# Weight rows in front of the merges, row blocks by turns and in-place combinations in a one-core adaLN kernel

## The chip, the cores and the metric

The kernel runs on one core of one Trainium2 chip. The metric is the device time of one execution in microseconds (us), given as a median of several executions. Lower is better.

## The reference

One adaLN layer over x of 4 batches x 1024 rows x 2048 columns, in float32. A modulation of six parts is made from a small vector, each part a 2048 x 2048 block of `wmod` ("a section"). A long convolution over the columns (a state-space kernel K with a skip term D), and then a linear layer whose weight is W plus sixteen LoRA updates, each stand between a layer norm with scale and shift and a gated residual.

```
mod = (silu(c) @ wmod).reshape(4, 6, 1, 2048)
sa, ca, ga, sb, cb, gb = six parts of mod            # sections 0 to 5
ga, gb = sign(g) * max(|g|, 0.25)
h = layernorm(x) * (1 + ca) + sa
x = x + ga * (causal_conv(h, K) + D * h)             # K from the state-space parameters
h = layernorm(x) * (1 + cb) + sb
x = x + gb * (h @ W.T + bias + sum_e coeffs_e * scales_e * (h @ A_e.T) @ B_e.T)
```

The inputs are random; some are scaled up by fixed factors.

## The kernel before

The work has three stretches. **Set-up**: K is computed and written as Toeplitz blocks, and sections 1, 0 and 2 of the modulation are made. **Convolution**: 16 groups of 256 rows (two row blocks of 128). **Linear layer**: two halves q of output columns by 16 units of 256 rows, with a seven-product scheme (Strassen-Winograd form), whose seven weight combinations were merged with the LoRA product and stored to a scratch tensor `wcd` during the convolution. Every matmul operand is split into a high and a low float16 part, and three of the four products are taken.

The program is written in order, and a framework then fixes at build time which instruction stands where in each engine's queue. It may move a ready instruction ahead of an earlier one that it expects to wait, and program order is the priority. On the chip each queue runs in its order. All large loads and stores are issued by SyncE's queue (SP).

**Modulation rows.** A section is 16 rows (L816 to L835): `mod_load` (L314) loads a [128, 2048] float32 tile of 1 MiB, tag `wm`, in a pool of three buffers (`WM, WMS = 3, 3`, L781), and `mod_mm` (L320) does four matmuls with it into one PSUM tile. A seventeenth step turns the sum into a column or gate. Each of these matmuls shows as two records in the trace, so a row is 8.

**LoRA preparation.** `prep_lora` (L385) loads A (`la`, 2 MiB) and then B (`lb`, 2 MiB) into the one buffer `we`, takes norms with ScalarE squares whose element output is junk (`lsq`, L412, tag `wct`), and writes the float16 factors `lbh` and `lbl` (L421 to L424).

**Merges.** `merge` (L429) does one of eight column chunks in 15 steps. Eight steps each make a PSUM tile `lps` of six matmuls (L448) and add it to the loaded weight on VectorE (L450). Squares (L458, junk `wsq` in `wct`), a power-of-two scale and two scaling steps follow. Then seven combinations of the quarters b11, b12, b21, b22 are written by `put` (L472): a ScalarE cast, a VectorE subtraction for the low part (L476), and a store from `wch`, of two buffers. One combination goes through an own tile `wct` (L483).

**Convolution of a group.** `conv_mm` (L552) goes over the output halves q = 0, 1 and in each over the row blocks r = 0, 1. For each it runs three `family` calls (L560): family 0 into `ya`, which ScalarE copies to `qs` (L585, one buffer); family 2 into `yb`, which VectorE adds to `qs` (L589) and gates (L591); and family 1 on top of `ya`, which VectorE gates (L597) and adds to the residual (L604). A family has 12 matmuls for q = 0 (512, 384, 256 and 128 columns, three each: "short") and 24 for q = 1 ("long"). `ya`, `yb` and `lps` share five PSUM tiles (`ACC = 5`, L772).

**Fill order.** Between families `tick()` is called, 18 times a group; `PLAN` (L775) says what comes at each. "S" takes one step of the generator `rest` (L884), from group 1 on. "P" and "Q" are the store and statistics of a finished row block (`conv_post`, L616), "T" and "N"/"O" prepare the next group (`stats`, `conv_prep` L521). The order inside `rest` is:

```
mods = (x for sec in (4, 3, 5) for x in section(sec, (wmp,)))
n = 0
for _ in mer:          # prep_lora, then eight merges
    yield
    n += 1
    if n % MR == 0:    # MR = 2
        next(mods, None)
        yield
for _ in mods:
    yield
```

So step 0 of group 1 is the LoRA preparation, step 1 the first merge matmuls, step 2 the first row of section 4. When `rest` is used up, its pools are closed (L916). Group 0 has no gate while it is convolved; the gate tile is made after it (L979) and `conv_late` (L608) applies it on VectorE, followed by the two stores `x1d` of `conv_post`.

Of the kernel before, what the change touches and what calls it, by code (L numbers as in the profile page):

```python
# [12 lines left out]
F32 = mybir.dt.float32  # L13
F16 = mybir.dt.float16
BF16 = mybir.dt.bfloat16
# [4 lines left out]
MUL, ADD, SUB = ALU.mult, ALU.add, ALU.subtract  # L20
# [4 lines left out]
P = 128  # L25
# [9 lines left out]
class Net:  # L35
# [349 lines left out]
    def prep_lora(self, pool, tmp):  # L385
        nc, v, io = self.nc, self.nc.vector, self.io
        ws = pool.tile([P, 2, 2], F32, tag="lws", name="lws")
        for i, n in enumerate(("coeffs", "scales")):
            x = io[n]
            for k in range(2):  # L390
                src = bass.AP(tensor=x.tensor, offset=x.offset + 8 * k, ap=[[1, 8], [0, 16], [1, 1]])
                nc.sync.dma_start(out=ws[:, i, k : k + 1], in_=src)
        a = tmp.tile([P, 2, D], F32, tag="we", name="la")
        nc.sync.dma_start(out=a, in_=io["A"].rearrange("c p k h d -> p c k (h d)"))

        am = pool.tile([P, 2], F32, tag="lam", name="lam")
        av = a.rearrange("p k d -> p (k d)").rearrange("p (c k d) -> p k c d", c=HC, k=2)
        for k in range(2):
            nc.scalar.activation(av[:, k], av[:, k], AF.Square, accum_out=am[:, k : k + 1])
        nc.scalar.activation(am, am, AF.Sqrt)  # L400
        sa, ia = self.pow2(pool, am, 2, "lsa")
        wt = pool.tile([P, 2], F32, tag="lwt", name="lwt")
        v.tensor_tensor(wt, ws[:, 0, :], ws[:, 1, :], MUL)
        v.tensor_tensor(wt, wt, ia, MUL)
        self.lsa = sa
        b = tmp.tile([P, 2, D], F32, tag="we", name="lb")
        nc.sync.dma_start(out=b, in_=io["BfT"].rearrange("(k p) o -> p k o", p=P))
        b4 = pool.tile([P, 4], F32, tag="lb4", name="lb4")
        for k in range(2):
            nc.scalar.activation(b[:, k], b[:, k], AF.Copy, scale=wt[:, k : k + 1])  # L410
            for h in range(2):
                j = tmp.tile([P, 1024], F32, tag="wct", name="lsq")  # L412
                i = 2 * k + h
                nc.scalar.activation(j, b[:, k, ds(1024 * h, 1024)], AF.Square, accum_out=b4[:, i : i + 1])
        bm = pool.tile([P, 1], F32, tag="lbm", name="lbm")
        v.tensor_reduce(bm, b4, AX.X, ADD)
        nc.scalar.activation(bm, bm, AF.Sqrt)
        sb, self.linv = self.pow2(self.cst, self.allmax(pool, bm, 1, "lbm"), 1, "lsb")
        self.bh = pool.tile([P, 2, D], F16, tag="lbh", name="lbh")
        self.bl = pool.tile([P, 2, D], F16, tag="lbl", name="lbl")  # L420
        for k in range(2):  # L421
            nc.scalar.activation(b[:, k], b[:, k], AF.Copy, scale=sb)
            nc.scalar.copy(self.bh[:, k], b[:, k])  # L423
            v.tensor_tensor(self.bl[:, k], b[:, k], self.bh[:, k], SUB)  # L424
        self.winv = self.const("winv", [P, NC])
        self.wcd = self.dram.tile([2, 7, P, HC, 2, 512], F16, tag="wcd", name="wcd")


    def merge(self, pool, tmp, c):  # L429
        nc, v = self.nc, self.nc.vector  # L430
        lf = tmp.tile([P, 2, 2, P], F32, tag="laf", name="laf")
        nc.sync.dma_start(out=lf, in_=self.io["A"][c])
        la = tmp.tile([P, 2, 2, 2, P], F16, tag="lac", name="lac")
        for k in range(2):
            v.tensor_scalar(lf[:, k], lf[:, k], self.lsa[:, k : k + 1], None, MUL)
        nc.scalar.copy(la[:, 0], lf)
        v.tensor_tensor(la[:, 1], lf, la[:, 0], SUB)
        we = tmp.tile([P, 2, D], F32, tag="we", name="we")
        for h in range(2):
            nc.sync.dma_start(out=we[:, h], in_=self.io["WT"][ds(P * (c + HC * h), P), :])  # L440
        for h in range(2):
            for q in range(4):
                ps = self.acc.tile([P, 512], F32, tag="a", name="lps")
                osl = ds(512 * q, 512)
                n = 0
                for k in range(2):
                    for x, y in ((0, self.bh), (0, self.bl), (1, self.bh)):
                        nc.tensor.matmul(ps, la[:, x, k, h], y[:, k, osl], start=(n == 0), stop=(n == 5))  # L448
                        n += 1
                v.scalar_tensor_tensor(we[:, h, osl], ps, self.linv, we[:, h, osl], MUL, ADD)  # L450
                yield

        m = pool.tile([P, 4], F32, tag="wem", name="wem")
        for h in range(2):
            for q in range(2):
                j = tmp.tile([P, 1024], F32, tag="wct", name="wsq")
                i = 2 * h + q
                nc.scalar.activation(j, we[:, h, ds(1024 * q, 1024)], AF.Square, accum_out=m[:, i : i + 1])  # L458
        mm = pool.tile([P, 1], F32, tag="wmm", name="wmm")
        v.tensor_reduce(mm, m, AX.X, ADD)  # L460
        nc.scalar.activation(mm, mm, AF.Sqrt)
        s, inv = self.pow2(pool, mm, 1, "wes")
        for h in range(2):
            v.tensor_copy(self.winv[:, c + HC * h : c + HC * h + 1], inv)
            for q in range(2):
                sl = ds(1024 * q, 1024)
                nc.scalar.activation(we[:, h, sl], we[:, h, sl], AF.Copy, scale=s)
            yield
        b11, b12 = we[:, 0, 0:1024], we[:, 0, 1024:2048]
        b21, b22 = we[:, 1, 0:1024], we[:, 1, 1024:2048]  # L470

        def put(i, t):  # L472
            hl = tmp.tile([P, 2, 2, 512], F16, tag="wch", name="wch", bufs=2)
            tv = t.rearrange("p (q n) -> p q n", n=512)
            nc.scalar.copy(hl[:, :, 0, :], tv)
            v.tensor_tensor(hl[:, :, 1, :], tv, hl[:, :, 0, :], SUB)  # L476
            STQ(nc).dma_start(out=self.wcd[:, i, :, c].rearrange("q p h n -> p q h n"), in_=hl)

        put(0, b11)
        put(1, b21)  # L480
        yield
        put(2, b22)
        t1 = tmp.tile([P, 1024], F32, tag="wct", name="wct")  # L483
        v.tensor_tensor(t1, b12, b11, SUB)
        put(4, t1)
        yield
        v.tensor_tensor(b12, b22, b12, SUB)
        put(6, b12)
        yield
        v.tensor_tensor(b11, b12, b11, ADD)  # L490
        put(5, b11)
        yield
        v.tensor_tensor(b21, b21, b11, SUB)
        put(3, b21)
        yield

# [55 lines left out]
    def conv_mm(self, pl, hs, xs, std, tick, early, out):  # L552

        nc, v = self.nc, self.nc.vector
# [19 lines left out]
                if i == 3 and q == 1:  # L574
                    tick()

        for q in range(2):
            for r in range(2):
                y = ys[r]
                yv = y.rearrange("p (j e t) -> p j e t", e=2, t=P)  # L580
                jj = slice(4 * q, 4 * q + 4)
                pa = self.acc.tile([P, 4, P], F32, tag="a", name="ya")
                family(pa, 0, q, r, True)
                qs = pl["q"].tile([P, 4, P], F32, tag="qs", name="qs")
                nc.scalar.copy(qs, pa)  # L585
                tick()
                pb = self.acc.tile([P, 4, P], F32, tag="a", name="yb")
                family(pb, 2, q, r, True)
                v.tensor_tensor(yv[:, jj, 1, :], pb, qs, ADD)  # L589
                if not early:  # L590
                    v.tensor_tensor(yv[:, jj, 1, :], yv[:, jj, 1, :], gv[:, jj, 1, :], MUL)  # L591
                tick()
                family(pa, 1, q, r, False)
                if early:
                    nc.scalar.copy(yv[:, jj, 0, :], pa)
                else:
                    v.tensor_tensor(yv[:, jj, 0, :], pa, gv[:, jj, 0, :], MUL)  # L597
                    self.residual(xs[r], ys[r], std[:, r : r + 1], sums[r], q)
                tick()

    def residual(self, x, y, std, sums, q):

# [165 lines left out]


ORDER = (0, 4, 5, 1, 6, 2, 3)  # L770
MR = 2
ACC, TPS = 5, 2  # L772


# [20 lines left out]
def net(ctx: ExitStack, tc: tile.TileContext, io):  # L795
    nc = tc.nc
# [12 lines left out]
    pl = {}  # L809
# [73 lines left out]
        pl[name] = pool(left, "p1" + name, bufs)  # L883
    def rest():  # L884
        mods = (x for sec in (4, 3, 5) for x in section(sec, (wmp,)))
        n = 0
        for _ in mer:
            yield
            n += 1
            if n % MR == 0:  # L890
# [4 lines that stand above are left out]
        k.ginv = k.fold_scale(msm, k.cb, k.sb, "fs2", k.winv)  # L895
        yield
# [179 lines left out]
```

## Time and profile before

| | us |
|---|---|
| Median of 3 executions | 2163.01 |
| Lowest, highest | 2156.66, 2166.04 |
| The profiled execution | 2160.88 |
| Its span, first to last instruction | 2159.1 |
| TensorE (PE) busy | 2070.2 |
| VectorE (DVE) busy | 1273.2 |
| ScalarE (ACT) busy | 912.2 |

The profile is of one execution. Its times count from the start of the span. PE is TensorE's matmuls and PEld its weight loads; SPq is SP's queue, whose lines are DMA issues and not the movement itself. Its part 2 cuts the span in 40 slices of 54 us with a digit for the busy tenths, and PEclk is the granted TensorE clock in tenths. A line of the order of time has start, duration, engine, source line, operation, output and inputs, count, and in brackets the idle time before it and what ended that.

Groups 1 to 15 of the convolution run from about 167 to 945 us, the linear layer from there to the end.

### The profile page before, as it was taken

How to read it: one execution, taken by the hardware profiler on the slowest of the kernel's cores; microseconds unless marked ns; L12 is line 12 of the kernel's file. 1: busy time of each engine (PE TensorE's matmuls, PEld its weight loads, DVE VectorE, ACT ScalarE, POOL GpSimd, SP SyncE). 2: the span in 40 equal slices, each digit the busy share in tenths (PEclk: the TensorE clock that was granted, in tenths of full speed). 3: DMA queues.
4: the chain of work that ended last, by engine and by line, in shares of the span. 5: the costliest groups of instructions: out<-in, count | busy, mean ns of one | idle time of the engine just before them, and what ended most of it. 6: DMA issues, size and time to landing. Idle time of an engine off the chain costs nothing.

```text
span 2159.1 us, 27722 instructions
## 1 busy us (share of the span) xinstructions
PE 2070.2 (96%) x11084; PEld 1020.6 (47%) x11084; DVE 1273.2 (59%) x2037; ACT 912.2 (42%) x1267; POOL 2.7 (0%) x12
## 2 busy tenths in 40 slices
PE   5696999999999999999999999999999999999999
PEld 1143554545445555654555555545444444444444
DVE  6537778887788877765666566565533323232323
ACT  1246666666667666654555454554200000000000
POOL 0000000000000000000000000000000000000000
PEclk8797999999999999999999999999999999999999
DMA  9987577876775442397556465465695545555542
GB/s 399 379 294 292 209 284 277 306 260 246 280 293 183 173 158 98 127 360 275 218 214 217 173 225 214 169 244 192 248 345 183 185 156 171 169 165 167 175 153 72
DMA packets 127130, 483.00 MB, mean 224 GB/s; under 512 B 13670, under 2 KB 13799, under 8 KB 96023
## 3 DMA queue, kind: packets, MB, share of 16 engines
q1 hardware_dynamic: 126464, 479.65, 61.7%
q8 instruction: 87, 1.43, 0.3%
q10 hardware_dynamic: 538, 1.59, 0.2%
q14 instruction: 41, 0.34, 0.0%
HBM read 325.89 MB, written 155.30 MB: 223 GB/s over the span
## 4 chain that ended last, share of the span: by engine, by line
PE 62%; issue 25%; DVE 7%; DMA 3%; ACT 3%; SPq 0%; POOL 0%; POOLq 0%; DVEq 0%; ACTq 0%
PE fZ L712 23%; PE fX L712 15%; PE fY L712 15%; PE ya L569 3%; PE tp L662 3%; PE yb L569 2%; PE modps L322 1%; DVE h L549 1%; ACT x L622 1%; DVE y L604 1%; ACT h L548 1%; DMA xo<-x1d 1%; DVE s4wr L177 1%; DMA w<-wcd 1%; DVE st L513 1%
## 5 line engine op out<-in xcount | busy, mean ns | idle before, releaser
L712 PEld LDWEIGHTS <-lf 128*128 128x128 f16 x5376 | 525.8, 98 | 620.2 <-issue 0.5
L712 PE MATMUL fZ<-w,lf 128*128 128x512 f16 x2304 | 514.0, 379 | 0.2 <-ACT p L720 0.2
L569 PEld LDWEIGHTS <-h 128*128 128x128 f16 x3456 | 319.7, 98 | 317.1 <-issue 69.1
L569 PE MATMUL ya<-kh,h 128*128 128x512 f16 (+3 forms) x1536 | 380.5, 328 | 8.2 <-ACT qs L585 5.1
L712 PE MATMUL fY<-w,lf 128*128 128x512 f16 x1536 | 343.1, 379 | 0.0
L712 PE MATMUL fX<-w,lf 128*128 128x512 f16 x1536 | 342.5, 379 | 0.0
L569 PE MATMUL ya<-kl,h 128*128 128x512 f16 (+3 forms) x768 | 251.5, 328 | 0.0
L731 DVE SCALAR_TENSOR_TENSOR xo<-xo,mv,gb 128x512 f32<-128x512 f32 x128 | 95.2, 750 | 248.7 <-DMA xo<-x1d 236.7
L569 PE MATMUL yb<-kh,h 128*128 128x512 f16 (+3 forms) x768 | 192.2, 326 | 0.0
L720 ACT COPY p<-fZ 128x512 f32<-128x512 f32 x64 | 37.3, 582 | 292.5 <-PE fZ L712 275.0
L322 PE MATMUL modps<-wm,sct 128*32 128x512 f32 x768 | 116.5, 677 | 43.1 <-DMA wm<-in_wmod 34.0
L664 ACT ACTIVATE gt<-tp,sb,cb 128x256 f32<-128x256 f32 x256 | 123.9, 570 | 63.7 <-PE tp L662 62.1
L720 ACT COPY p<-fX 128x512 f32<-128x512 f32 x32 | 18.7, 586 | 303.9 <-PE fX L712 240.2
L542 ACT ACTIVATE t<-tp,sa,ca 128x256 f32<-128x256 f32 x256 | 126.2, 565 | 32.3 <-PE tp L539 23.4
L549 DVE TENSOR_TENSOR h<-t,h 128x1536 f16<-128x1536 f32 x64 | 112.2, 1754 | 28.2 <-ACT h L548 27.7
L569 PE MATMUL yb<-kl,h 128*128 128x512 f16 (+3 forms) x384 | 125.2, 326 | 0.0
L548 ACT CAST h<-t 128x1536 f16<-128x1536 f32 x64 | 94.1, 1470 | 26.2 <-DVE t L547 26.2
L736 DVE TENSOR_TENSOR fin<-fX,gb 128x512 f32<-128x512 f32 x32 | 22.1, 692 | 125.8 <-PE fX L712 125.7
L448 PE MATMUL lps<-lbh,lac 128*128 128x512 f16 x256 | 87.2, 382 | 6.4 <-ACT lbh L423 5.1
L675 DVE TENSOR_TENSOR lf<-gt,lf 128x1024 f16<-128x1024 f32 x64 | 76.7, 1220 | 18.3 <-ACT lf L674 18.2
L513 DVE BATCH_NORM_STATS2 st<-x 128x6 f32<-128x512 f32 x128 | 83.3, 681 | 5.1 <-DMA x<-in_x 5.1
L539 PE MATMUL tp<-ident,x 128*128 128x128 f32 x512 | 73.0, 279 | 12.8 <-ACT t L542 6.9
(236 smaller groups left out, 1863.1 us busy)
## 6 DMA issues: line engine op xcount, KB each, us to landing
wm<-in_wmod SPq DMA_DIRECT2D x96, 1024.0 KB
lfd<-lf SPq DMA_DIRECT2D x112, 512.0 KB
lf<-lfd SPq DMA_DIRECT2D x112, 512.0 KB
x<-in_x SPq DMA_DIRECT2D x32, 1024.0 KB
x1d<-y SPq DMA_DIRECT2D x32, 1024.0 KB
x<-x1d SPq DMA_DIRECT2D x32, 1024.0 KB
xo<-x1d SPq DMA_DIRECT2D x128, 256.0 KB
out<-xo SPq DMA_DIRECT2D x128, 256.0 KB
```

Source lines behind the costliest of these rows:

```text
L322: self.last = self.nc.tensor.matmul(self.modps[32 * g : 32 * g + 32, :], self.sct[:, j].rearrange("p r b -> p (r b)"), w[:, ds(512 * g, 512)],
L448: nc.tensor.matmul(ps, la[:, x, k, h], y[:, k, osl], start=(n == 0), stop=(n == 5))
L513: v.bn_stats(st[:, q], xs[r][:, ds(512 * q, 512)])
L539: nc.tensor.transpose(tp[:, c, r], xs[r][:, ds(P * (4 * k + 2 * i + c), P)], self.ident)
L542: nc.scalar.activation(t[:, 2 * i + c], tp[:, c], AF.Identity, bias=self.sa[:, d, b : b + 1], scale=self.ca[:, d, b : b + 1],)
L548: nc.scalar.copy(h[:, 0], t)
L549: v.tensor_tensor(h[:, 1], t, h[:, 0], SUB)
L569: nc.tensor.matmul(pf[:, o:512], h[:, x], self.kf[f][z][:, ds(k0, 512 - o)], start=first, stop=(i == last and (x, z) == (1, 0)), skip_grou ...
L664: nc.scalar.activation(t[:, c0 + c], tp[:, c], AF.Identity, bias=self.sb[:, c0 + c, b : b + 1], scale=self.cb[:, c0 + c, b : b + 1],)
L675: v.tensor_tensor(hl[:, :, 1, :], s, hl[:, :, 0, :], SUB)
L712: nc.tensor.matmul(ps[name], lf[i][:, k, x, :], wc[i][k // 4][:, k % 4, y, :], start=(first and n == 0), stop=(n == 3 * HC - 1), skip_grou ...
L731: v.scalar_tensor_tensor(x, x, m, self.gbias[:, h], ADD, ADD)
```

## The change

Six edits, which come together:

1. `rest` takes ten rows of section 4 first. After the seventh it takes one step of the merge generator, which is the LoRA preparation.
2. After that one row follows three merge steps, not two (`MR` 3).
3. In the half q = 0, the two row blocks take turns: family 0 of both, family 2 of both, family 1 of both. Half q = 1 keeps its order. The number of ticks stays 18. `qs` has a buffer for each row block.
4. The combinations are made in place in b12 and b11, and the tile `wct` of 4 KiB a partition goes. Products 5 and 6 are stored in the other order.
5. The junk of the squares goes to bfloat16 views of `wch` tiles.
6. The pool of weight tiles has three buffers, as it had.

```diff
-                j = tmp.tile([P, 1024], F32, tag="wct", name="lsq")
+                j = tmp.tile([P, 2, 2, 512], F16, tag="wch", name="lsq", bufs=2)
+                j = j.rearrange("p q h n -> p (q h n)").bitcast(BF16)[:, 0:1024]
...
-        t1 = tmp.tile([P, 1024], F32, tag="wct", name="wct")
-        v.tensor_tensor(t1, b12, b11, SUB)
-        put(4, t1)
+        v.tensor_tensor(b12, b12, b11, SUB)
+        put(4, b12)
         yield
         v.tensor_tensor(b12, b22, b12, SUB)
-        put(6, b12)
-        yield
-        v.tensor_tensor(b11, b12, b11, ADD)
-        put(5, b11)
-        yield
-        v.tensor_tensor(b21, b21, b11, SUB)
+        put(5, b12)
+        yield
+        v.tensor_tensor(b11, b12, b11, SUB)
+        put(6, b11)
+        yield
+        v.tensor_tensor(b21, b21, b12, SUB)
         put(3, b21)
...
-        for q in range(2):
-            for r in range(2):
...
+        def begin(q, r):
+            pa = self.acc.tile([P, 4, P], F32, tag="a", name="ya")
+            family(pa, 0, q, r, True)
+            qs = pl["q"].tile([P, 4, P], F32, tag=f"qs{r}", name="qs")
+            nc.scalar.copy(qs, pa)
+            tick()
+            return pa, qs
...
+        ps = [begin(0, r) for r in range(2)]
+        for r in range(2):
+            odd(0, r, ps[r][1])
+        for r in range(2):
+            even(0, r, ps[r][0])
+        for r in range(2):
+            pa, qs = begin(1, r)
+            odd(1, r, qs)
+            even(1, r, pa)
...
-MR = 2
+MR, MOD0 = 3, 10
...
         mods = (x for sec in (4, 3, 5) for x in section(sec, (wmp,)))
+        for n in range(MOD0):
+            if n == MOD0 - 3:
+                next(mer)
+                yield
+            next(mods)
+            yield
         n = 0
```

`odd` and `even` hold the statements of families 2 and 1 as they were, and the squares of the merges (`wsq`) get the same edit as `lsq`.

More of the change, by code (lines that the diff above doesn't have):

```diff
@@ L455, in merge @@
             for q in range(2):
-                j = tmp.tile([P, 1024], F32, tag="wct", name="wsq")
+                j = tmp.tile([P, 2, 2, 512], F16, tag="wch", name="wsq", bufs=2)
+                j = j.rearrange("p q h n -> p (q h n)").bitcast(BF16)[:, 0:1024]
                 i = 2 * h + q
@@ L575, in family @@
                     tick()
-        for q in range(2):
-            for r in range(2):
[L579 to L599, printed above, removed]
+        def begin(q, r):
[5 more added lines that the diff above has]
+            return pa, qs
@@ new lines, in odd, with even @@
+        def odd(q, r, qs):
+            yv, jj = ys[r].rearrange("p (j e t) -> p j e t", e=2, t=P), slice(4 * q, 4 * q + 4)
+            pb = self.acc.tile([P, 4, P], F32, tag="a", name="yb")
+            family(pb, 2, q, r, True)
+            v.tensor_tensor(yv[:, jj, 1, :], pb, qs, ADD)
+            if not early:
+                v.tensor_tensor(yv[:, jj, 1, :], yv[:, jj, 1, :], gv[:, jj, 1, :], MUL)
+            tick()
+        def even(q, r, pa):
+            yv, jj = ys[r].rearrange("p (j e t) -> p j e t", e=2, t=P), slice(4 * q, 4 * q + 4)
+            family(pa, 1, q, r, False)
+            if early:
+                nc.scalar.copy(yv[:, jj, 0, :], pa)
+            else:
+                v.tensor_tensor(yv[:, jj, 0, :], pa, gv[:, jj, 0, :], MUL)
+                self.residual(xs[r], ys[r], std[:, r : r + 1], sums[r], q)
+            tick()
```

## The prediction

> **What bounds the kernel now.** I read the busy shares and the slices first, then a table by stretches, then PE's waits, then the order of time on PE and on SP's queue at the one hole. Page, parts 1 and 2:
>
> ```profile
> PE 2070.2 (96%) x11084; PEld 1020.6 (47%) x11084; DVE 1273.2 (59%) x2037; ACT 912.2 (42%) x1267; POOL 2.7 (0%) x12
> ...
> PE   5696999999999999999999999999999999999999
> ...
> PEclk8797999999999999999999999999999999999999
> ```
>
> TensorE is the bound: 2070 of 2159 us, and nearly all of the other 89 us lies in the first four slices (54 us each). Slices 1 to 3 are fed by the weight rows of sections 1, 0 and 2, which the change doesn't touch. The fourth (162 to 216 us) is its subject. The stretches around it, as us of busy time per engine, then granted clock and DMA share:
>
> ```profile
> 167.00:177.90 10.90, 10.86 (x74) 5.57 (x72) 10.87 (x16) 6.56 (x11) 0.00 (x0) 1.00 0.93 362
> 177.90:199.80 21.90, 1.93 (x3) 0.29 (x4) 16.03 (x46) 19.78 (x23) 0.40 (x1) 0.57 0.87 348
> 199.80:206.00 6.20, 6.20 (x22) 2.82 (x22) 5.53 (x9) 2.96 (x4) 0.00 (x0) 0.60 0.15 24
> ...
> 400.00:690.00 290.00, 282.76 (x1750) 147.20 (x1749) 240.01 (x419) 195.19 (x269) 0.00 (x0) 1.00 0.71 261
> 690.00:945.00 255.00, 246.02 (x1537) 143.34 (x1536) 199.46 (x370) 169.11 (x230) 0.38 (x1) 1.00 0.45 166
> ```
>
> One hole of 21.9 us with 1.93 us of PE work; later PE is 97% busy. Its two causes, on PE:
>
> ```profile
> 175.08 2.78 PE L322 MATMUL modps<-wm,sct 128*32 128x512 f32 x24
> 192.81 1.92 PE L322 MATMUL modps<-wm,sct 128*32 128x512 f32 x2 [14.95 <-DMA wm<-in_wmod]
> 199.79 0.58 PE L448 MATMUL lps<-lbh,lac 128*128 128x512 f16 x1 [5.06 <-ACT lbh L423]
> 200.17 0.63 PE L569 MATMUL ya<-kh,h 128*128 128x512 f16 x1
> ```
>
> Three rows of section 4 run (24 records), the fourth waits 15 us for its load, then the first merge matmul waits 5 us for the LoRA factor lbh. Behind both, in queue order, stands group 1's second row block (200.17), whose inputs had long been ready. Why the fourth row came late, on SP's queue:
>
> ```profile
> 170.50 0.38 SPq L407 DMA_DIRECT2D lb<-in_BfT  x1
> 176.07 4.59 SPq L618 DMA_DIRECT2D x1d<-y  x2
> 180.76 2.56 SPq L502 DMA_DIRECT2D x<-in_x  x2
> 183.41 0.99 SPq L317 DMA_DIRECT2D wm<-in_wmod  x2
> ```
>
> Its slot was not free before the rows of 175.08 had run, and SP then stood at group 0's stores (the second waits for DVE until 180.3) and x loads. The other PE waits, whole run:
>
> ```profile
> PE ya L569 <- ACT qs L585: 5.1, 8, 1.8
> PE lps L448 <- ACT lbh L423: 5.1, 1, 5.1
> PE ya L569 <- DVE y L589: 2.8, 1, 2.8
> ...
> PE lps L448 <- DVE y L589: 1.3, 1, 1.3
> ```
>
> The qs waits (5.1 here; the page's group of L569 has 8.2 us of idle in all) are what taking turns aims at. The two on DVE y L589 look like waits for a PSUM tile to be emptied.
>
> **What the Trainium skill says.** "PSUM — Partial Sum Buffer", section "Engine vs sequencer instructions": matmuls start and complete in program order, and the ScalarE and VectorE queues are strict FIFO. The trace agrees: ready matmuls stood 20 us behind one row. "TensorE: Matmul & The Clock Gate", section "What's actually happening": after an idle window of about 3.4 us the array runs at half clock until it has been busy about as long. The trace has 0.57 in the hole and 0.60 in the 6.2 us after it. "DMA: Bandwidth & Descriptors", section "Issuing engines are not separate DMA queues": all queues share the same 16 engines, so loads compete. Here the share is 0.93 at 362 GB/s before the hole. "Perfetto Trace Analysis", section "Identifying Performance Opportunities", takes regular gaps as a possible sign of too few PSUM buffers. Here they are few: 10 us of 442 from 248 to 690.
>
> **The change part by part.** The sum is made against the profiled execution: 2160.9 us (span 2159.1 and 1.8 around it); the median of three, 2163.0, lies 2.1 above.
>
> *Rows in front of the merges.* In front of the first merge matmul the fill order now has seven rows, the LoRA preparation, then three rows; that matmul becomes step 11 of group 1, not step 1. What the hole costs today: 20.0 us idle, plus 6.2 x 0.40 = 2.5 us at half clock after it, plus 0.9 us because the row at 192.81 took 1.9 us where one takes 1.0 at full clock: **23.4 us**.
>
> What PE can run there: a short family takes 1.73 us (173.35 to 175.08). Group 1's second block has three: 5.2 us. Its long families (24 matmuls) take 4.2 us (217.82 to 222.04) and may start when the last h piece is written, 182.8; three of them give 12.6 us. Seven rows (3 to 9) give 7 us. The sum, 24.8 us, covers 20. No work is added: the 48 rows are all loaded anyway.
>
> What stays is whether the rows arrive. With 10.9 us of work as now up to 177.9, 5.2 of short families, 3 for rows 3 to 5, two long families 8.4, rows 6 to 8, a transpose piece 0.9 and half a family 2.6, PE wants row 9 at about 201. From 157 on DMA has to move 10 rows, lb (2 MB), two x1d and two x tiles, each of 1 MiB: 16 x 1.05 = 16.8 MB, at 362 GB/s 46 us, so until 203: 2 us short. And the rows pass SP's queue behind the x1d stores and x loads (176.07 to 183.41, 7.3 us): I take half, 4 us. Row 0 now runs earlier, after the first short family, so its slot frees about 169, and some reloads get ahead of the stores. Residual wait **+6**, bounds 0 (all in time) and 13.2 (row 3 still lands at 192.8 and PE reaches it at 177.9 + 1.73 = 179.6). Half clock after shorter waits: **+1.5**, bounds 0 and 3.4, today's.
>
> The LoRA chain (la square at 166.6, lb load at 170.5, ACT at 182.87 to 199.7) keeps its instructions; its step moves from 0 to 7, so its six loads on SP, ACT's some 20 instructions and one POOL reduction rank behind more group 1 work. lbh at 200 to 205 is hidden as PE reaches the merges only past 201: 0; without that cover up to +5.
>
> *Merges by threes.* With one row after three merge steps (was two) a group's 18 steps hold 13.5 merge steps, not 12. A merge costs DVE (46.0 + 57.6 + 9.8 + 39.0 + 5.5 + 5.3)/8 = 20.4 us for its lines L450, L476, L484 to L493, L437, L435, so 1.36 per step and +2.0 us per group. A group takes about 49 us with DVE 83% busy (240 of 290): it becomes 87%. PE is the later engine, so this is hidden; it costs only where PE waits for DVE. The fill ends after 173 steps, not 182, still in front of group 15 where it is needed: 0.
>
> *Turns in the short half.* Same matmuls, same 18 ticks. Family 1 of a block now stands three short families, 5.2 us, behind its qs copy (0.58 us), not one: its wait goes. Half of the 8.2 us are from long families or other causes: **-3**, bounds 0 and -8. The price is PSUM: ya and yb of both blocks, four of five accumulators, are open at once, so merges have one or two tiles, not three. lps (1.3 us) and its DVE pass (0.74) recur every tick of about 3 us, so one tile is enough unless DVE's queue is late. With the denser merges I take **+4**, bounds 0 and +38 (two waits of 2.1 us, the mean of the two DVE y waits above, in 8.9 groups).
>
> *In place, and squares into wch.* The operation count is the same. b12 is written again only after put(4) has read it (1.04 ACT + 1.22 DVE), one step later anyway: 0; without cover 2.3 us x 8 = 18 us on DVE, not on PE. The squares write 2-byte junk: ACT's 1057 ns stay. They take slots whose last store stands on SP ahead of the next weight load (274.14 against 274.55): no new wait. The second qs tile takes no time.
>
> **Sum:** -23.4 + 6 + 1.5 - 3 + 4 = -14.9 us: 2146.0 for a profiled execution, 2148 with the 2.1.
>
> **Rivals.**
> *Rows still late.* SP keeps today's order, row 3 lands at 192.8: 13.2 us of the hole stay, with today's half-clock cost, and later rows lose 2 us as their slots free late. Gain 20.0 - 13.2 = 6.8, less 2; with the -3 and +4 that leaves 3.8: 2157.1, so **2159**. For it: DMA at 0.93 and SP standing at 176 to 183. Against: row 0's earlier turn.
> *PSUM and DVE, slower.* In the short halves PE waits for a tile twice a group, 2.1 us each, in 8.9 groups with merges: +37.4. With the other terms (-18.9): 2179.4, so **2181**. For it: four open accumulators, DVE at 87%. Against: two such waits today in all, 4.1 us. It gets slower by over 0.5% from 29.7 us, 3.3 us a group.
> *Nothing left.* The hole closes but lbh is late by 5 and PSUM waits take 12: so -23.4 + 6 + 1.5 - 3 + 5 + 12 = -1.9: **2161**.
>
> **How the numbers follow.** Forecast 0.55 with all that is faster by over 0.5%; late rows 0.18 and nothing left 0.10, both within 0.5%; slower 0.17. A measurement of this kernel tells about 0.5% (10.8 us) from no change, so faster is below 2152.2. The range: low 2134, all of 23.4 and some qs waits gained; high 2174, the edge of no change; outside stay the slower rival's 0.17 and 0.03 below.
>
> **What would show it.** Right: no PE gap over 6 us past 178; a short family of the second block straight after the first's; the first lps past 200; clock 1.0 from 200 to 206; no qs waits in short halves. Wrong: a row waiting over 10 us for wm; lps or ya waiting for DVE y more than ten times; PE under 97% from 248 to 690.

## The result and the profile after

| us | before | after |
|---|---|---|
| Median (20 executions each) | 2162.27 | 2166.34 |
| Lowest to highest | 2156.66 to 2166.04 | 2163.73 to 2170.0 |
| The profiled execution, its span | 2160.88, 2159.1 | 2163.73, 2161.9 |
| First gate matmul to first matmul of the linear layer, same profiles | 772.7 | 772.2 |

The ratio is 1.0021 with an interval of 1.0014 to 1.0029: slower by about 4 us, and within the 0.5% that the prediction called no change. It forecast 2148. The last row is the convolution (`gps`, the gate tile's first matmul, at 165.73 and 169.33; `fX` at 938.45 and 941.53). It is 0.5 us shorter. The profile's 2.8 us more lie ahead of it, where the gate came 3.6 us later. In the profiles of the kernels below the gate comes anywhere from 166.05 to 171.18, without a clear link to the edits, so I judge the change by the convolution and by the medians. The convolution is known from one profiled execution of each kernel, and that execution lies up to some 5 us from the kernel's median (2168.69 against 2173.94 in one case below); differences of a few us between convolutions alone say little.

Parts 1 and 2 of the page after:

```profile
PE 2080.0 (96%) x11084; PEld 1022.9 (47%) x11084; DVE 1271.9 (59%) x2037; ACT 912.3 (42%) x1267; POOL 4.1 (0%) x12
...
PE   5699899999999999999999999999999999999999
...
PEclk8699999999999999999999999999999999999999
```

The fourth slice has gone from 6 to 9, as forecast, and its clock from 7 to 9. The fifth (216 to 270 us) has gone from 9 to 8. The table by stretches (busy us of PE, PEld, DVE, ACT, POOL, then clock, DMA share, GB/s) shows the exchange. First the changed kernel, then two stretches of the kernel before:

```profile
177.90:199.80 21.90, 21.90 (x146) 10.71 (x144) 19.61 (x42) 10.96 (x15) 0.00 (x0) 1.00 0.97 364
199.80:206.00 6.20, 5.34 (x36) 1.97 (x35) 5.61 (x17) 2.48 (x3) 0.00 (x0) 1.00 1.01 424
206.00:216.00 10.00, 6.43 (x32) 2.89 (x36) 1.76 (x9) 10.00 (x11) 0.00 (x0) 0.66 1.03 420
216.00:248.00 32.00, 23.21 (x112) 10.48 (x105) 19.43 (x28) 22.55 (x31) 1.86 (x1) 0.84 0.64 243
...
400.00:690.00 290.00, 282.52 (x1714) 147.26 (x1713) 244.28 (x421) 198.73 (x275) 0.00 (x0) 1.00 0.71 265
690.00:945.00 255.00, 246.84 (x1554) 143.18 (x1553) 200.25 (x369) 167.12 (x225) 0.38 (x1) 1.00 0.42 153
```

```profile
206.00:216.00 10.00, 10.00 (x57) 5.21 (x56) 6.01 (x9) 4.72 (x5) 0.00 (x0) 1.00 0.47 197
216.00:248.00 32.00, 32.00 (x194) 16.85 (x195) 18.12 (x35) 20.38 (x32) 0.00 (x0) 1.00 0.40 140
```

The old hole, 178 to 200, is full. A new one stands behind it: PE is idle for 0.86 + 3.57 + 8.79 = 13.2 us from 199.8 to 248, and its clock drops to 0.66 and 0.84, which by the table's own figures costs an estimated 6.43 x 0.34 + 23.21 x 0.16 = 5.9 us. In the kernel before, the stretches 206 to 248 were busy throughout at full clock. So 23.4 us became 19.1, a gain of 4.3, of which the convolution shows 0.5.

Most of the rest went into the rows themselves. From the gate to the linear layer PE is idle for 7.0 us less than before (32.0, not 39.0), but with the same number of matmul records it is busy for 6.5 us more (740.2, not 733.7). The 48 rows take 59.0 us of this, where they took 53.7. Most of the reason shows in the first row of section 4 in the changed kernel:

```profile
174.54 1.04 PE L322 MATMUL modps<-wm,sct 128*32 128x512 f32 x2
175.52 1.09 PE L540 MATMUL tp<-ident,x 128*128 128x128 f32 x8
176.54 1.06 PE L322 MATMUL modps<-wm,sct 128*32 128x512 f32 x6
```

A row's four matmuls write four different groups of 32 partitions of one PSUM tile, and here they overlap: a whole row (8 records) takes 1.07 us, its first matmul alone (2 records) 1.04, the other three (6 records) 1.06. Where the order that was fixed at build time puts other matmuls behind the first one, the row costs a microsecond more. Two rows are split in this way in the kernel before and seven in the changed one; five more are an estimated 5 us. No run changes these splits alone.

From 400 on the shares of the stretches hardly moved. PE's order of time in the new hole:

```profile
203.95 1.07 PE L322 MATMUL modps<-wm,sct 128*32 128x512 f32 x8
205.88 0.44 PE L540 MATMUL tp<-ident,x 128*128 128x128 f32 x2 [0.86 <-ACT x L529]
207.87 0.88 PE L540 MATMUL tp<-ident,x 128*128 128x128 f32 x6 [1.55 <-ACT x L529]
210.76 2.02 PE L540 MATMUL tp<-ident,x 128*128 128x128 f32 x8 [2.02 <-ACT t L543]
212.72 4.38 PE L322 MATMUL modps<-wm,sct 128*32 128x512 f32 x24
222.09 2.02 PE L540 MATMUL tp<-ident,x 128*128 128x128 f32 x8 [4.99 <-ACT t L543]
...
230.41 0.58 PE L449 MATMUL lps<-lbh,lac 128*128 128x512 f16 x1 [3.59 <-ACT lbh L424]
```

By 205 PE has run nine of group 1's twelve families and seven of the ten rows. What comes next in its order is group 2's transposes, which need group 2's normalised x (L529) and whose PSUM tiles ScalarE empties (t, L543), with the other three rows among them (212.72), and then the first merge matmul, which wants lbh. Only behind that stand the last three long families of group 1. Before, the first such transposes ran at 228.9, behind 29 us of families and merge matmuls. The three rows at 212.72 take 4.38 us at the lower clock; 24 such records took 2.78 us at 175.08 before. What ScalarE does meanwhile:

```profile
203.73 4.08 ACT L529 ACTIVATE x<-x,nb,rs 128x2048 f32<-128x2048 f32 x2 [1.30 <-DVE nb L519]
...
211.60 3.90 ACT L410 ACTIVATE lb<-lb,lwt 128x2048 f32<-128x2048 f32 x2
...
219.55 1.47 ACT L549 CAST h<-t 128x1536 f16<-128x1536 f32 x1
...
224.67 3.90 ACT L423 ACTIVATE lb<-lb,lsb_s 128x2048 f32<-128x2048 f32 x2
228.47 3.69 ACT L424 CAST lbh<-lb 128x2048 f16<-128x2048 f32 x2
```

The 16 us block for B (two scaling passes, four squares, a cast, from 211.60) stands between the copies out of PSUM that the transposes wait for, and lbh's cast is reached at 228.47. It doesn't explain all of PE's waits: the first three, 0.86 + 1.55 + 2.02 = 4.4 us, end before the block starts, while ScalarE is normalising group 2's x and squaring a finished block (L637, 207.72). The wait of 4.99, one of 0.21 after it and the 3.59 for lbh, 8.8 us in all, stand behind it. Before, the block ran while PE stood in the old hole, and the x of group 2 came after it:

```profile
182.87 1.99 ACT L410 ACTIVATE lb<-lb,lwt 128x2048 f32<-128x2048 f32 x1
...
197.86 3.68 ACT L423 CAST lbh<-lb 128x2048 f16<-128x2048 f32 x2
...
205.44 4.08 ACT L528 ACTIVATE x<-x,nb,rs 128x2048 f32<-128x2048 f32 x2
```

Link by link the LoRA chain fell behind: A's load from 151.87 to 166.71 (+14.8), its first square from 166.57 to 179.85 (+13.3), B's load from 170.50 to 190.59 (+20.1), B's scaling from 182.87 to 211.60 (+28.7), the cast +30.6. In each of these, 3.6 us are the later gate of this profile.

### The profile page after: what moved, and what is told of

Same layout as the page of the kernel before. It is cut to its first block, busy times and chain, and to the rows that moved or that the text cites. A ratio compares the mean times of both kernels' runs of the same rounds, so it can differ in the third digit from the quotient of the medians.

```text
span 2161.9 us, 27708 instructions
## 1 busy us (share of the span) xinstructions
PE 2080.0 (96%) x11084; PEld 1022.9 (47%) x11084; DVE 1271.9 (59%) x2037; ACT 912.3 (42%) x1267; POOL 4.1 (0%) x12
## 4 chain that ended last, share of the span: by engine, by line
PE 64%; issue 23%; DVE 8%; ACT 3%; DMA 2%; ACTq 0%; POOL 0%; POOLq 0%; SPq 0%; DVEq 0%
PE fZ L727 23%; PE fX L727 15%; PE fY L727 15%; PE ya L570 3%; PE tp L677 2%; PE modps L322 2%; PE yb L570 1%; DVE h L550 1%; DVE st L514 1%; DVE y L619 1%; ACT x L529 1%; ACT x L637 1%; DVE s4wr L177 1%; PE tp L540 1%; ACT t L543 1%
## 5 line engine op out<-in xcount | busy, mean ns | idle before, releaser
L322 PE MATMUL modps<-wm,sct 128*32 128x512 f32 x768 | 123.7, 698 | 27.4 <-DMA wm<-in_wmod 18.8
L543 ACT ACTIVATE t<-tp,sa,ca 128x256 f32<-128x256 f32 x256 | 126.9, 570 | 27.8 <-PE tp L540 14.5
```

The source lines that it names most:

```text
L322: self.last = self.nc.tensor.matmul(self.modps[32 * g : 32 * g + 32, :], self.sct[:, j].rearrange("p r b -> p (r b)"), w[:, ds(512 * g, 512)],
L543: nc.scalar.activation(t[:, 2 * i + c], tp[:, c], AF.Identity, bias=self.sa[:, d, b : b + 1], scale=self.ca[:, d, b : b + 1],)
```

## The experiments

Two theories. **M**: the step of `rest` that holds the LoRA preparation was moved behind seven rows, so its ScalarE block and lbh come 30 us later and the hole moves with them. **G**: the turns, with four open PSUM tiles, or the denser merges give back what the rows gain. Ratios are to the kernel before, with their intervals; "convolution" is the stretch of the last table row, 772.7 before and 772.2 after. PE's waits in the hole are those from 170 to 250 us; the changed kernel has 7.2 for `t`, 3.6 for lbh and 2.4 for `x`. Diffs are against the changed kernel, except where said.

**Rows alone.** The kernel before with the ten rows and `MR` 3; its convolution and merges stay as they were.

```diff
-MR = 2
+MR, MOD0 = 3, 10
...
+        for n in range(MOD0):
+            if n == MOD0 - 3:
+                next(mer)
+                yield
+            next(mods)
+            yield
```

> Rows and threes alone: the fill order of the change (ten rows, the LoRA preparation as its eighth step, then one row after three merge steps), with the convolution order and the merges of before. Theory M (the LoRA preparation is moved with the rows, its ScalarE block and lbh come 30 us later, and the hole moves with them): 2162 to 2168, lbh near 228, a PE hole between 200 and 230. Rival G (turns and PSUM give back what the rows gain): about 2147, the hole closed.

Measured: 2165.45, ratio 1.0011 [1.0004, 1.0019]; convolution 773.7, lbh's cast at 228.40, PE waiting 7.0 us for `t`, 4.0 for lbh and 2.2 for `x`. Without turns and without in-place combinations the result is the same: M holds, and G's 2147 doesn't.

**All but the rows.**

```diff
-MR, MOD0 = 3, 10
+MR, MOD0 = 2, 0
```

> Everything of the change but the rows: turns, in-place combinations and junk into wch, with no rows in front and one row after two merge steps, as before. M: 2157 to 2163, the hole at 178 to 200 back where it was before, perhaps shorter by the second block's short families (up to 5 us). G: about 2177, with the give-back and without the gain.

Measured: 2167.17, 1.0017 [1.0008, 1.0026]; convolution 775.7. The old hole is back on PE:

```profile
195.28 1.94 PE L322 MATMUL modps<-wm,sct 128*32 128x512 f32 x8 [13.32 <-DMA wm<-in_wmod]
...
202.64 0.58 PE L449 MATMUL lps<-lbh,lac 128*128 128x512 f16 x1 [5.42 <-ACT lbh L424]
```

Neither number was met. The turns and in-place edits gain nothing by themselves; the kernel is some 4 us slower with them, far from G's 2177. Where these 4 us come from was not traced.

**Preparation first, then the rows.**

```diff
-            if n == MOD0 - 3:
+            if n == 0:
                 next(mer)
```

> The change with the LoRA preparation as the first step of group 1, as before, then the ten rows, then the merges. M: lb is loaded near 170 and lbh is ready near 200 again, while rows and both blocks' families fill PE: 2145 to 2152, no PE wait above 6 us between 170 and 240. G: no change against the changed kernel, 2163 to 2170.

Measured: 2156.29, 0.9972 [0.9963, 0.998]; convolution 764.0, 8.2 us less than in the changed kernel. This one line turns the loss into a gain and beats both kernels. M's direction holds, but 4 to 11 us of the gain that it expected are missing. Its stretches, and the ScalarE and VectorE lines at the hole that is left:

```profile
177.90:199.80 21.90, 20.51 (x135) 10.26 (x137) 21.03 (x53) 18.96 (x22) 0.40 (x1) 1.00 0.91 354
199.80:206.00 6.20, 2.77 (x16) 0.20 (x8) 5.32 (x11) 4.91 (x6) 0.00 (x0) 0.65 1.01 428
206.00:216.00 10.00, 7.21 (x44) 3.23 (x44) 1.13 (x5) 8.44 (x10) 0.00 (x0) 0.71 1.00 363
216.00:248.00 32.00, 30.23 (x176) 14.90 (x173) 19.63 (x34) 14.99 (x26) 0.00 (x0) 1.00 0.68 265
```

```profile
198.74 3.68 ACT L424 CAST lbh<-lb 128x2048 f16<-128x2048 f32 x2
...
206.06 4.08 ACT L529 ACTIVATE x<-x,nb,rs 128x2048 f32<-128x2048 f32 x2 [0.56 <-DVE nb L519]
```

```profile
200.65 4.49 DVE L425 TENSOR_TENSOR lbl<-lb,lbh 128x2048 f16<-128x2048 f32 x2 [1.09 <-ACT lbh L424]
205.06 0.16 DVE L71 RECIPROCAL rs<-r_t 128x2 f32<-128x2 f32 x1
```

lbh is back at 198.74 and no merge waits for it. PE is idle for 9.4 us from 177.9 to 248 (in the changed kernel 13.2), and the clock costs 3.1 by the same working: 12.4 in all, where the changed kernel has 19.1. Five rows are split, not seven. The longest wait is 4.1 us for group 2's normalised x (L529), whose reciprocal standard deviation stood on VectorE behind the subtraction for lbl; rows for their loads cost 2.9. That x comes at about the time at which it came before the change (205.44); PE is there sooner.

**Merges by twos.**

```diff
-MR, MOD0 = 3, 10
+MR, MOD0 = 2, 10
```

> The change with one row after two merge steps, as before, in place of three. M: 2164 to 2169, the hole at 205 to 230 unchanged. G, in the form that the denser merges load VectorE: 2158 to 2162, with fewer PE waits past 248.

Measured: 2173.94, 1.005 [1.0034, 1.0066]; convolution 778.7. The hole is unchanged (7.3 us for `t`, 4.0 for lbh), and PE is busy for 277.4 us from 400 to 690, where the changed kernel has 282.5. Both expectations were missed. With ten rows already done, threes cost nothing: they save 6 us by the ratios, 7.6 by the medians, and G's term for denser merges has the wrong sign.

**Only A's loads early.** `prep_lora` becomes a generator, its first two loads issued ahead of the rows, the rest after the seventh row as in the change.

```diff
         nc.sync.dma_start(out=a, in_=io["A"].rearrange("c p k h d -> p c k (h d)"))
+        yield
...
+            if n == 0:
+                next(mer)
             if n == MOD0 - 3:
```

> The change with only the LoRA preparation's first loads (coeffs, scales, A) issued ahead of the ten rows; its arithmetic and the load of B keep their place after the seventh row. Theory M-queue (SP's order alone, 15 us of the delay of A, makes the chain late): lbh near 212, 2154 to 2159. Theory M-rank (all of the preparation ranks behind group 1's work on ScalarE, VectorE and SP): lbh past 222, 2161 to 2167. G: 2163 to 2170.

Measured: 2165.29, 1.0014 [1.0007, 1.0021]; convolution 774.0. A's load is back at 152.32 and its squares start at 166.90, but B's load still goes out at 185.13 and lbh's cast runs at 224.66. As the form M-rank said, it is the rank of the whole preparation that counts, and not SP's order at A's load.

**Preparation ahead of group 0's convolution.** The rows then start at step 0.

```diff
         for n in range(MOD0):
-            if n == MOD0 - 3:
-                next(mer)
-                yield
             next(mods)
...
     take(sec, 16)
+    next(mer)
```

> The change with the whole LoRA preparation ahead of group 0's convolution in program order, behind the rows of section 2. M: lb is loaded 5 to 10 us earlier than in the version with the preparation first in group 1, lbh is ready by 195, ScalarE is free for group 2's preparation at 200: 2145 to 2152, no PE wait above 3 us between 170 and 230. Against it: its VectorE work stands in front of group 0's late gate and delays the stores and the x loads: then 2156 to 2162. G: 2163 to 2170.

Measured: 2162.53, 0.9999 [0.9991, 1.0008]; convolution 771.3. lbh's cast is at 196.22, only 2.5 us earlier than with the preparation first in group 1, because B's load still waits for its buffer until 171.29. Now group 0's work is pushed: its stores are issued at 178.45 (176.39 with the preparation first), group 2's x loads at 189.01 (181.07), its normalised x comes at 211.49, and PE waits 4.7 us for a qs copy. Earlier is not better without end: it is 6 us slower than the preparation first in group 1, and the work that it overtook is later. M's number was missed; the one against it, 2156 to 2162, was nearly met.

**Six rows, preparation first.**

```diff
-MR, MOD0 = 3, 10
+MR, MOD0 = 3, 6
...
-            if n == MOD0 - 3:
+            if n == 0:
```

> The LoRA preparation first in group 1, then six rows, then the merges (ten rows in the version before it, which took 2156). M: the first merge matmuls come four steps earlier, at about the time at which lbh is ready (200), and fill the 8 us hole in which PE waited for group 2's normalised x: 2146 to 2152. If lbh is later than PE by over 5 us it is no gain: 2155 to 2160. G: 2160 to 2168.

Measured: 2159.16, 0.9986 [0.9978, 0.9994]; convolution 767.8. The first merge matmul runs at 205.84, after a wait of 4.9 us for `lac`, and 4.0 us go to a qs copy: 8.9 us of waits, where ten rows with the preparation first leave 9.3. Fewer rows leave as much; M's 2146 to 2152 was missed.

**B's squares on VectorE.**

```diff
-                nc.scalar.activation(j, b[:, k, ds(1024 * h, 1024)], AF.Square, accum_out=b4[:, i : i + 1])
+                bb = b[:, k, ds(1024 * h, 1024)]
+                v.scalar_tensor_tensor(j, bb, 1.0, bb, MUL, MUL, accum_out=b4[:, i : i + 1])
```

> The change with the four LoRA squares of B on VectorE, which idles there, in place of ScalarE: 5 us less of ScalarE's block in front of group 2's preparation, the chain to lbh as long as it was. M: the 5.0 us wait of the transposes near 222 shrinks by 4 or 5 us, 2160 to 2163. If only lbh matters and not what stands behind the block: no change, 2165 to 2168. G: no change.

Measured: 2167.48, 1.0021 [1.0009, 1.0032]; convolution 777.35. M's expectation was missed, and the time is that of "no change". The cast runs at 225.98, 2.5 us earlier, and the wait for lbh became one of 6.5 us for lbl on VectorE, with 5.5 us for `t` left. So shortening ScalarE's block by moving part of it to VectorE, also in lbl's chain, gained nothing.

**No turns, preparation first.** The kernel of "rows alone" with the preparation first.

```diff
-            if n == MOD0 - 3:
+            if n == 0:
                 next(mer)
```

> The kernel before with ten rows and one row after three merge steps, the LoRA preparation kept first: as the version that took 2156, but without turns and in-place combinations. M (place of the preparation decides, turns matter little): 2154 to 2159. G (turns give back what the rows gain): about 2145.

Measured: 2155.88, 0.9966 [0.9953, 0.9979]; convolution 769.0. The same as with turns (2156.29) within the intervals. With the preparation first, turns and in-place combinations together neither give nor cost anything that can be measured.

**Merges by fours, preparation first.**

```diff
-MR, MOD0 = 3, 10
+MR, MOD0 = 4, 10
...
-            if n == MOD0 - 3:
+            if n == 0:
```

> The version with the preparation first in group 1 and ten rows, with one row after four merge steps, not three. If the loss of 8 us from threes to twos goes on the same way (merges that end earlier help): 2149 to 2154. If three is enough and denser merges load VectorE: 2156 to 2162. M says nothing on it beyond an unchanged stretch up to 250.

Measured: 2159.08, 0.9981 [0.9974, 0.9988]; convolution 769.8. Not better than three.

**Preparation after three rows.**

```diff
-            if n == MOD0 - 3:
+            if n == 3:
```

> The change with the LoRA preparation after three rows (before the first row took 2156, after the seventh is the change, 2166). M-rank: in between, 2157 to 2164, lbh between 205 and 222. If only SP's order of the loads of A and the first three rows counts: as the change, 2164 to 2168.

Measured: 2164.83, 1.0004 [0.9996, 1.0012]; convolution 775.0. B's load at 189.03, lbh's cast at 221.16, 6.3 us of waits for `t` and 6.9 for `x`. Three rows in front cost nearly as much as seven. lbh fell where M-rank said, the time where its rival said, though SP's order of A's load was no cause in the run with A's loads early. Of the places tried, only the first in group 1 brings the gain.

**A shorter block, left where the change puts it.**

```diff
-            nc.scalar.activation(b[:, k], b[:, k], AF.Copy, scale=wt[:, k : k + 1])
...
-                nc.scalar.activation(j, b[:, k, ds(1024 * h, 1024)], AF.Square, accum_out=b4[:, i : i + 1])
+        v.memset(b4, 1.0)
...
-            nc.scalar.activation(b[:, k], b[:, k], AF.Copy, scale=sb)
```

> The change with part of the LoRA preparation left out: B is neither scaled by its weights, nor squared, nor scaled again, and its norm is taken as a constant, so ScalarE's block is 12 us shorter at the same place in the order and lbh needs only A's chain, B's load and the casts. M: lbh near 212 to 218, the PE wait for it and the 5 us wait of group 2's transposes gone, 2152 to 2158. G: 2163 to 2170.

This kernel leaves out B's scalings and the norm of B, so it computes something else. Measured: 2155.79, 0.9969 [0.9957, 0.9981]; convolution 765.8. With 12 us less of ScalarE work the time falls by 10.5 us (11 by the ratios), though every step keeps its place. Its lines in the stretches of the hole, and its cast:

```profile
206.00:216.00 10.00, 4.79 (x22) 2.26 (x22) 5.27 (x8) 10.00 (x13) 0.00 (x0) 0.56 0.66 270
216.00:248.00 32.00, 30.94 (x170) 14.46 (x171) 20.46 (x28) 13.92 (x23) 0.00 (x0) 0.92 0.76 290
```

```profile
210.26 3.69 ACT L417 CAST lbh<-lb 128x2048 f16<-128x2048 f32 x2
```

PE's 23.21 us from 216 to 248 become 30.94, and no merge waits for lbh. From 199.8 to 248 PE is idle for 8.1 us (13.2 in the changed kernel), and the clock costs 4.6: 12.7 in all, not 19.1. The 6.4 us between them are what the convolution gains, and nearly the 6.7 that the preparation in the first place takes off the hole. So these 12 us of the displaced block make about a third of the new hole; why the medians show 10.5 us, the profiles don't tell. The run shortens the block and the chain to lbh at once, so it doesn't separate the two.

The last three runs, the second of them at the change's place, ask about the 9.4 us that are left with the preparation first: ScalarE's block, or VectorE's queue?

**Scalings folded, preparation first.** B's two scaling passes go into the squares, the cast and the subtraction.

```diff
-            nc.scalar.activation(b[:, k], b[:, k], AF.Copy, scale=wt[:, k : k + 1])
...
-                nc.scalar.activation(j, b[:, k, ds(1024 * h, 1024)], AF.Square, accum_out=b4[:, i : i + 1])
+                nc.scalar.activation(j, b[:, k, ds(1024 * h, 1024)], AF.Square, scale=wt[:, k : k + 1], accum_out=b4[:, i : i + 1])
...
-            nc.scalar.activation(b[:, k], b[:, k], AF.Copy, scale=sb)
-            nc.scalar.copy(self.bh[:, k], b[:, k])
-            v.tensor_tensor(self.bl[:, k], b[:, k], self.bh[:, k], SUB)
+            nc.scalar.activation(self.bh[:, k], b[:, k], AF.Copy, scale=ws2[:, k : k + 1])
+            v.scalar_tensor_tensor(self.bl[:, k], b[:, k], ws2[:, k : k + 1], self.bh[:, k], MUL, SUB)
```

> The version with the preparation first in group 1 and ten rows (2156), with B's two scaling passes folded into the squares, the cast and the subtraction: ScalarE's block is 7.9 us shorter, VectorE's work the same. If the rest of the hole is ScalarE's block: lbh near 192 to 195, group 2's x normalised before 203, 2147 to 2152. If it is VectorE's queue or the load of group 2's x: 2154 to 2158.

Measured: 2157.2, 0.9966 [0.9952, 0.9979]; convolution 767.8. As the second expectation said, 7.9 us less on ScalarE bring nothing here. ScalarE then stands idle for 6.28 us until VectorE delivers, and VectorE has the subtraction in the midst of group 2's statistics:

```profile
208.01 0.20 ACT L70 ACTIVATE r_t<-r_v 128x2 f32<-128x2 f32 x1 [6.28 <-DVE r_v L69]
```

```profile
199.66 0.63 DVE L514 BATCH_NORM_STATS2 st<-x 128x6 f32<-128x512 f32 x1
200.21 4.59 DVE L425 SCALAR_TENSOR_TENSOR lbl<-lb,lw,lbh 128x2048 f16<-128x2048 f32 x2
204.72 1.87 DVE L514 BATCH_NORM_STATS2 st<-x 128x6 f32<-128x512 f32 x3
```

**Scalings folded, at the change's place.** The same fold, the preparation after seven rows.

> The changed kernel with the same folding, the preparation still after the seventh row. M: like the version with B's norm left out (2156, 12 us less), scaled to 7.9 us less: 2157 to 2162, lbh near 220. G: 2163 to 2170.

Measured: 2164.18, 0.9997 [0.9988, 1.0005]; convolution 773.3. The wait for lbh is gone (cast at 220.66), but 7.8 us of waits for `t` stay. The medians put the gain at 2 us, the ratios at 5, of the 7.9 us saved; M expected 2157 to 2162. M was missed: two thirds of the shorter block's saving bring less than half of its gain. Without a wait for lbh much of the loss stays, so lbh alone doesn't make it.

**The subtraction on GpSimd, preparation first.**

```diff
-            v.tensor_tensor(self.bl[:, k], b[:, k], self.bh[:, k], SUB)
+            nc.gpsimd.tensor_tensor(self.bl[:, k], b[:, k], self.bh[:, k], SUB)
```

> The version with the preparation first in group 1 and ten rows (2156), with the two lbl subtractions (4.5 us) on GpSimd instead of VectorE. If VectorE's queue holds group 2's x: its normalisation starts 3 to 4 us earlier (206 before), the 4.1 us wait of the transposes shrinks to about 1, 2151 to 2154. If ScalarE (free at 202.3) or the rows' loads hold it: 2155 to 2159.

Measured: 2163.55, 0.9999 [0.9989, 1.0009]; both expectations missed. The subtraction took 8.08 us on GpSimd, and VectorE stood still beside it:

```profile
205.59 8.08 POOL L425 TENSOR_TENSOR lbl<-lb,lbh 128x2048 f16<-128x2048 f32 x2 [9.07 <-issue]
```

```profile
206.66 3.02 DVE L75 TENSOR_TENSOR r_v<-r_v,rs 128x2 f32<-128x2 f32 x1
209.71 3.98 DVE L76 TENSOR_TENSOR r_t<-r_t,r_v 128x2 f32<-128x2 f32 x1
```

These two take 0.16 us each elsewhere. They hold group 2's normalised x until 214.12, and PE waits 8.53 us for it. The run brought a stall of its own, so it doesn't tell whether VectorE's queue alone makes the rest of the hole. That stays open.

## Why the prediction was wrong, point by point

**What bounds, and where the hole is: right.** PE is the bound, the old hole's two causes were the fourth row and lbh, and both come back when the rows are taken out again (13.3 and 5.4 us).

**Rows in front: right for the old hole.** From 177.9 to 199.8 PE is busy for all 21.9 us, by the work that was named: short and long families of group 1 and rows. The residual wait of +6 for rows didn't come: no row waits in the changed kernel's hole (the waits there are all for ScalarE), and the "rows still late" rival fell with it. With the preparation first, rows wait 2.9 us. Half clock (+1.5) was absent before 206 and cost 5.9 us after it.

**"No work is added": wrong in what the work takes.** The 48 rows are the same, but seven of them are split, not two, and they take 5.3 us more of PE. One of the two before is the "row" at 192.81 itself: it was the first matmul alone, and the other three ran at 229.82.

**The LoRA chain, and what PE reaches next: the step that failed.** The prediction saw that the chain's loads and some 20 ScalarE instructions "rank behind more group 1 work", and then priced lbh at "200 to 205 is hidden as PE reaches the merges only past 201: 0; without that cover up to +5". Measured, lbh's cast starts at 228.47. For the hole as a whole it left 6 + 1.5 us; the new one costs 19.1. Two things went wrong in it.

First, the delay: each link was taken to keep its time, though the step that issues it moved; the runs show the chain adding 14.8 us at A's load, 20.1 at B's, 28.7 where it enters ScalarE. Preparation first puts the cast back to 198.74, takes the hole to 12.4 us and the time from 2166 to 2156.

Second, who is hit: only the merge that uses lbh was asked after. Of PE's 13.2 us of waits in the hole 9.6 are group 2's transposes, which don't use the chain at all. The sum has "a transpose piece 0.9" ahead of row 9 at 201, without a wait, though in the kernel before the x for it is normalised on ScalarE only from 205.44. So 4.4 of the 9.6 us come before the block, because PE is there too soon; the other 5.2 stand behind the chain's block on ScalarE. The shorter block fits: 12 us fewer on that queue, 6.4 off the hole, 10.5 off the time.

The view that would have told it was there: ScalarE's 19.78 busy us in the old hole. That hole was not empty time: for most of it ScalarE did the preparation. A fill that lets PE go on without it also brings PE to group 2's transposes 23 us sooner (205.9, not 228.9), and uses up families that stood in front of them.

**Merges by threes (0, and part of the +4): wrong sign of a small term.** Twos with the rows in front cost 7.6 us; fours instead of threes give 2159 instead of 2156. The waits on `DVE y` for lps are few, so a busier DVE was no limit there.

```profile
PE lps L449 <- DVE y L590: 3.1, 3, 2.2
...
PE ya L570 <- ACT qs L582: 0.2, 1, 0.2
```

**Turns (-3 for qs, +4 for PSUM): mechanism right, size near zero.** In these PE waits of the changed kernel (248 to 1000 us) the qs waits have gone from 5.1 us to 0.2, and the three lps waits are 3.1 us where the kernel before had one of 1.3. With and without turns, 2156.29 and 2155.88: the two terms cancel or are too small to see there. Without the rows in front, turns and in-place edits together cost some 4 us, which was not traced to either term. The slower rival (2181), which needed two waits of 2.1 us in every group, is refuted.

**In place and the squares' junk: 0, not tested apart.** They are there wherever the turns are and absent without them, and with the preparation first both ways give the same time.

**The sum and the rivals.** "Nothing left", 2161, came nearest to 2166.3, and its first term was right, but neither of its prices was: lbh's lateness was not 5 us at the merges but a displaced block on ScalarE, and the PSUM waits of 12 didn't come. None of the rivals had the mechanism that acted. The signs didn't tell either: PE's longest gap past 178 is 5.0 us, the first lps runs at 230.4, the clock is 1.00 from 200 to 206 and the qs waits are down to one of 0.2, all as for a right forecast, and none of the three signs of being wrong came. No sign asked for the transposes or for the clock after 206. The two rivals within 0.5%, given 0.28 together, have the size of the result by luck: for other reasons than those that acted.

**What stays open:** the 9.4 us of idle PE that remain with the preparation first, which a ScalarE block shorter by 7.9 us alone didn't reduce (4.1 of them are the wait for group 2's x); the 3.6 us by which the profiled gate came later, and with it where the 4 us of the medians lie; why the time gains 10 us with the preparation first, where hole (6.7) and splits (2) explain some 9; and the 4 us of the turns without the rows.

## What to carry to other kernels

A hole on one engine can be the time in which another engine does work that is needed soon. Before you fill it, list what the other queues do in it, give each of these steps its new start in the new order, and ask what the filled engine reaches next and what stands in front of it on each queue. Fill the hole around the chain that ends it and leave that chain's issue where it was: here the change took 4 us more with the chain behind seven of the ten rows and 6 us less with it first (by the ratios). And look whether matmuls that overlap still stand together in the new order: a row that was split took 2.1 us of PE, not 1.07.

## What was not expected of the hardware

Two VectorE instructions of two elements a partition took 3.02 and 3.98 us, against 0.16 elsewhere, while GpSimd did an elementwise subtraction of two SBUF tiles (two instructions, 205.59 to 213.67), and ended within 0.03 us of GpSimd's. The Trainium skill, page "SBUF — State Buffer", section "Who interferes with whom", says that the two engines share a port pair as an exclusive lock, and that VectorE instructions with two SBUF inputs contend for it. The trace agrees, as a reciprocal with one input beside GpSimd's first instruction took its usual 0.17 us.
